# The first outer set of group 0 on raw x: layer normalisation moved behind four products' results

## Chip, cores and metric

The kernel runs on one core of a Trainium2 chip, in fp32. The metric is the device time of the whole program in microseconds, median over runs. The engines are TensorE (PE, with its weight loads PEld), VectorE (DVE), ScalarE (ACT), GpSimd (POOL) and the queue engine SyncE (SP), which here issues nearly all DMAs. Each engine works through its own instructions in the order in which the program issued them.

## The reference

`x` is 2048 rows (tokens) by 512 features. With LN(v) the row-wise normalisation without weights:

```python
xn = layernorm(x)                                   # (v - mean) / sqrt(var + 1e-5), per token
s  = xn @ (weight * block_mask).T                   # 512 x 512, 32 x 32 blocks kept or not
nx = xn * rsqrt(mean(xn * xn) + 1e-5) * ln_w
h  = silu(nx @ gate_w.T) * (nx @ up_w.T)            # 1792 inner features
g  = silu(h @ down_w.T)                             # back to 512
out = x + s * g
```

The kernel leaves the second (RMS) normalisation out of the products: its factor is applied to s at the end, and `ln_w` is multiplied into the weight tiles.

## The kernel before, in words

**Tiles.** P is 128, W is 512. The kernel works on transposed data: features on the 128 partitions, 512 tokens along a tile. x has four token groups t of 512 tokens (four tiles i of 128 tokens each) and four feature chunks c of 128. A product is one matmul of a 128x128 weight block by a 128x512 operand. All buffers in SBUF are slots of 128x512 in one large tile `mem`, cut into named rings; `F[...]` is the first slot of a ring.

**Strassen-like sets.** Gate and up weights are handled in seven groups g, and the masked 512x512 matrix is an eighth (g = G). Each group's product is a 2x2 block product, computed by seven block products ("outer" set q = 1, 2, 6, 5, 7, 3, 4), and each of those again by seven matmuls m (1, 5, 2, 6, 3, 7, 4 in order of issue). One pair (g, q) is an `instance`, and its number j is its place in the order: first (0,1), (0,2), (1,1), (1,2), (2,1) and so on, sets 1 and 2 of all groups, then the other five sets of each group. Instance 0 is (g=0, q=1), instance 1 is (0,2), instance 4 is (2,1).

**The order of work** is written out by hand: `at(pos, fn)` files a piece of work under a position, and at the end all pieces are issued in order of position. Instance j has its seven matmuls at positions 7j + (0, 2, 3, 4, 6, 8, 12), so neighbours interleave, and one position stands for 0.86 us. The dictionary `EARLY` moves single events of the first instances. `T(us)` turns a time into a position; it is written as a planned time of the head and only sets the order.

**An instance** (L333) adds its products up in three PSUM banks X, Y, Z. Bank X takes m = 1, 6, 7, 4 one after another and is read in between: after m = 1 (copied to seed Z, or, in the first instances, to a slot `s1`), after 6 (snapshot `s2`), after 7 (sum with `s5`, the result 3), after 4 (result 2). Bank Y takes m = 5 (snapshot `s5`) and 3. A matmul that adds into a bank waits for the reading before it. The snapshot or sum is a ScalarE copy if there is no prior tile, else a VectorE addition. PSUM has three X banks, two Y, one Z and two others (V), for transposes and gate values.

**The head.** `load_x(0)` brings the 512 tokens of t = 0 as four tiles, then come weight blocks `load_a` (L249) and the other tokens, all on SP's queue in that order; a one-column GpSimd copy (L685) makes the loads behind the first x tile wait for it. VectorE computes mean and variance (`stats`, L123), `factors` (L128) gives scl = 1/sqrt(var + eps) and nb = -mean * scl for each token, `normalise` (L142) applies them in place on ScalarE and VectorE, TensorE transposes 128x128 blocks (L155), and `evacuate` (L158) copies each PSUM bank to a `raw` slot on ScalarE. Weight blocks are multiplied by ln_w (`scale_a`, L266), and GpSimd forms their sums (`inner_a`, L312: s1, s2, s4, s3). `inner_b` (L211) forms the operands' differences for m = 5, 6, 7, 4, the first three on VectorE and the last on GpSimd. Until the first product TensorE multiplies the identity by itself (L702, 26 times).

**After sets 1 and 2 of a group** instance (g,1) has left its four tiles in `acc`, and (g,2), with `acc` as prior, its four in `c1`: the 2x2 results of gate (tiles 0, 1) and up (2, 3) for two token groups n. `done` (L420) then issues, for each n, a silu on ScalarE into a V bank, and `h_out` (L413), a VectorE multiplication of silu and up tile, followed by a store to `h_dram`. `acc` is stored to `acc_dram` and read back for the later sets of the group.

**At the end** x is added from `x_t`, the transposed x in memory, cut by rows and columns.

Of the kernel before, what the change touches and what calls it, by code (L numbers as in the profile page):

```python
# [31 lines left out]
def tile_masked_linear_gated_ffn(  # L32
# [21 lines left out]
    rms_dram = tc.dram_tile([NT], F32, name="rms_dram")  # L54
    acc_dram = tc.dram_tile([G + 1, P, 4, W], F32, name="acc_dram")
# [49 lines left out]
    keep = const.tile([P, 4, 16], F32, tag="keep", name="keep")  # L105

    def constants():
        make_identity(nc, ident)
        nc.gpsimd.memset(blockones, 0.0)
        for b in range(P // BLK):  # L110
            nc.gpsimd.memset(blockones[b * BLK : (b + 1) * BLK, b * BLK : (b + 1) * BLK], 1.0)


    xt, raw, stat = {}, {}, {}
    agg = small.tile([P, NTT, TT, 2], F32, tag="agg", name="agg", bufs=1)
    rms = small.tile([P, NTT, TT], F32, tag="rms", name="rms", bufs=1)

    def load_x(t):
        for i in range(TT):
            xt[t, i] = mem[:, first_slot[("B6", "vc", "v5", "B4")[t]] + i, :]  # L120
            nc.sync.dma_start(xt[t, i], x[(t * TT + i) * P : (t * TT + i + 1) * P, :])
# [6 lines left out]
    def factors(t):  # L128


        scl = small.tile([P, TT], F32, tag="scl", name=f"scl_{t}")
        nb = small.tile([P, TT], F32, tag="nb", name=f"nb_{t}")
# [193 lines left out]

    def weights(g, q, m):
        if q < 3 and m in (1, 2, 4):
            return aq[g, 0, q - 1][:, {1: 0, 2: 2, 4: 3}[m] * P :][:, :P]
        return aop[g, q][m]  # L330


    def instance(j, g, q, prior, dest, after):  # L333
# [4 lines left out]
        seeded = j > 1  # L338

        def mm(m, tag, key, first):  # L340
            if first and key not in st:
                st[key] = bank("Y" if key == "z" and j == 1 else tag, f"{key}_{j}")
            nc.tensor.matmul(st[key], weights(g, q, m), operand(q, m), start=first and not (key == "z" and seeded),  # L343
                             stop=True, skip_group_check=True)

        def seed():
# [4 lines left out]
            else:  # L351
                st["s1"] = slot("s2" if j else "s5", f"s1_{j}")
# [22 lines left out]
        at(EARLY.get((j, 0), 7 * j + 1), seed)  # L375
        for off, m, tag, first, snapshot, out in (
# [9 lines left out]
            at(EARLY.get((j, m), pos), mm, m, tag, key, first)  # L386
            if snapshot:
                at(pos + 1, snap, key, *snapshot)
            elif out:

                pos += 2.3 if prior is None and m == 2 and seeded else 1
                if m == 2:
                    pos = EARLY.get((j, "z"), pos)
                at(pos, total, key, *out)
                after(out[1], pos)


    def group(g, where):
# [56 lines left out]
        }  # L455
        for q in setup:
            instance(where[g, q], g, q, *setup[q])

# [7 lines left out]
        at(7 * where[g, 1] + 15, lambda: nc.sync.dma_start(acc_dram[g], sums))  # L466
# [91 lines left out]
    def load_final(R, Hh, i, slot_s, slot_x):  # L558
# [6 lines left out]
        nc.sync.dma_start(fin[m, t][1], x_t[m * P : (m + 1) * P, t * W : (t + 1) * W])  # L565
# [18 lines left out]
    def down_instance(o, q, where_, prior, dest, after):  # L584
# [78 lines left out]
        if last_set:  # L663
            at(where_(17) + 0.1, base_of_last)
            for part, pos in zip(parts, (where_(23), where_(24), where_(25))):
# [11 lines left out]
    T = lambda us: (us - 14.0) / 0.86  # L677
    EARLY.update({(0, 1): T(10.4), (0, 2): T(11.3), (1, 1): T(12.1), (1, 2): T(13.0), (0, 0): T(11.5), (1, 0): 4.3,
                  (0, "z"): 3.26, (1, "z"): 4.9})
    SILU = 26.2  # L680
    at(T(-10), constants)
    at(T(-10), load_x, 0)
    at(T(-10), lambda: nc.scalar.dma_start(lnw_sb, ln_w))

    at(T(-10), lambda: nc.gpsimd.tensor_copy(mem[:, F["a1"], 0:1], xt[0, 0][:, 0:1]))  # L685
    for K in range(2):
        at(T(-10), load_a, 0, K)
# [16 lines left out]
    at(T(1.4), lambda: warm(26, bank("V", "idle")))  # L704
    for t, p, step in ((0, T(7.1), 0), (1, T(12.5), 0), (2, 36.0, 1.2), (3, 36.1, 1.2)):
        plan(p, step, factors(t))
    for i in range(TT):
        half = act if i < 2 else dve
        at(T(3.7 + 0.82 * i), stats, 0, i)
        at(T(9.35 + 0.82 * i), stats, 1, i)  # L710
        for h, cols in enumerate((slice(0, W // 2), slice(W // 2, W))):
            at(T(7.95 + 0.9 * h + 0.4 * (i % 2)), normalise, 0, i, half, cols)
            at(T(13.45 + 0.9 * h + 0.4 * (i % 2)), normalise, 1, i, half, cols)
        for c in range(KC):
            at(T((8.9, 9.3, 9.8, 11.0)[c] + 0.05 * i), transpose, 0, c, (2, 3, 0, 1)[i], "XYYX"[c])
            at(T((14.35, 14.8, 15.25, 16.2)[c] + 0.05 * i), transpose, 1, c, (2, 3, 0, 1)[i], "XVVV"[c])
    at(T(6.0), scale_a, 0, 0, pool)
    at(T(6.1), scale_a, 0, 1, pool)
    for c in range(KC):
        at(T((9.75, 10.3, 10.85, 12.05)[c]), evacuate, 0, c, act)  # L720
        at((5.6, T(15.6), 6.0, 3.14)[c], evacuate, 1, c, act)
    for pos, q, m, eng in ((1.1, 1, 5, dve), (1.87, 1, 6, dve), (2.56, 1, 7, dve), (3.95, 2, 5, dve), (2.7, 1, 4, pool),
                           (4.6, 2, 6, dve), (7.2, 2, 7, dve), (5.0, 2, 4, pool)):
        at(pos, inner_b, q, m, eng)
    for q in (1, 2):
        for k in (0, 1):
            for n in (0, 1):
                at(8, outer_b, q, k, n, None)
    at(2.1, scale_a, 1, 0)
    at(5.2, scale_a, 1, 1)  # L730
    for i in range(TT):
        at(14.0 + 2.5 * i, stats, 2, i)
        at(25.0 + 3 * i, stats, 3, i)
        at((44.0, 51.0, 55.2, 58.2)[i], normalise, 2, i, act)
        at(40.5 + 2.4 * i, normalise, 3, i, dve)
    plan(36.2, 1.2, rms_factor())
# [24 lines left out]
    for g in range(G + 1):  # L761
# [8 lines left out]
        if g:  # L770
            plan(p - 7, 1, inner_a(g, 1))
        else:
            plan(T(9.9), 0, inner_a(0, 1, 0, 1))
            plan(T(11.9), 0, inner_a(0, 1, 1, 1))
# [150 lines left out]
```

## Time and profile before

| | us |
|---|---|
| median of 3 runs (lowest, highest) | 513.35 (513.21, 513.50) |
| profiled execution | 513.17 |
| its span, first to last instruction | 511.4 |
| TensorE busy (matmul records) | 505.8 |
| VectorE, ScalarE, GpSimd busy | 380.4, 182.6, 340.9 |
| warm-up on the identity | 1.35 to 10.3 |
| first product | 11.48 |
| DMA mean rate over the span | 238 GB/s |
| DMA rate 10 to 18 us, then 20 to 24 us | 377 to 404 GB/s, 0 |

How to read it: an fp32 product shows as two matmul records. Records overlap in the pipeline, so the sum of their durations is more than the time they take; what a product costs is read from the distance between starts. Names such as L97 are line numbers; L97 is the helper `add`, through which all elementwise sums go, so its rows are told apart by engine, tiles and shape. "idle before" is the time in which an engine stood still before an instruction, with what released it.

### The profile page before, as it was taken

The numbers are of one execution on the slowest core, as the hardware profiler recorded it, in microseconds if no ns is written. First come the engines' busy times: TensorE is split into PE (matmuls) and PEld (weight loads), VectorE is DVE, ScalarE is ACT, GpSimd is POOL, SyncE is SP. The second block draws the span as 40 slices with busy tenths as digits, with TensorE's granted clock in tenths as the row PEclk, the third lists the DMA queues.
The fourth block names the chain that finished last, engine by engine and source line by source line (L and its number), as shares of the span: only waits on it lengthen the run. The fifth ranks groups of instructions, "written<-read, shape, count | busy, mean of one in ns | idle before, by whom it ended". The sixth has DMA issues, their size and how long they took to land. (4 is left out here: it accounts for less than half of the span.)

```text
span 511.4 us, 4943 instructions
## 1 busy us (share of the span) xinstructions
PE 505.8 (99%) x1269; PEld 231.8 (45%) x1269; DVE 380.4 (74%) x590; ACT 182.6 (36%) x348; POOL 340.9 (67%) x283
## 2 busy tenths in 40 slices
PE   8999999999999999999999999999999999999997
PEld 8444444444444444444444444444444444444444
DVE  6878689876977969699696978968747645367736
ACT  4656754633536353353634433330100101001111
POOL 5522224994795968869597789976662754739960
PEclk9999999999999999999999999999999999999999
DMA  8436636369159386785948667499997698476472
GB/s 289 164 132 238 247 133 227 135 236 350 48 219 348 147 302 228 238 289 208 338 166 294 209 239 254 169 332 383 357 339 270 204 374 327 146 252 216 151 229 83
DMA packets 60460, 121.59 MB, mean 238 GB/s; under 512 B 5760, under 2 KB 13328, under 8 KB 58384
## 3 DMA queue, kind: packets, MB, share of 16 engines
q1 hardware_dynamic: 60288, 121.27, 66.8%
q8 instruction: 10, 0.16, 0.1%
q14 instruction: 18, 0.15, 0.1%
q10 hardware_dynamic: 144, 0.00, 0.0%
HBM read 75.11 MB, written 46.15 MB: 237 GB/s over the span
## 5 line engine op out<-in xcount | busy, mean ns | idle before, releaser
L97 POOL TENSOR_TENSOR mem<-mem 128x512 f32<-128x512 f32 (+4 forms) x245 | 305.2, 1267 | 135.4 <-ACT mem L264 36.5
L343 PE MATMUL x<-mem 128*128 128x512 f32 x448 | 213.6, 595 | 0.2 <-DVE mem L97 0.2
L343 PEld LDWEIGHTS x<-mem 128*128 128x128 f32 x448 | 83.7, 190 | 107.3 <-issue 86.9
L97 DVE TENSOR_TENSOR mem<-x,mem 128x512 f32<-128x512 f32 x137 | 92.5, 684 | 42.0 <-PE x L343 41.1
L343 PE MATMUL y<-mem 128*128 128x512 f32 x224 | 114.5, 593 | 0.3 <-DVE mem L97 0.3
L97 DVE TENSOR_TENSOR mem<-mem 128x512 f32<-128x512 f32 (+3 forms) x60 | 74.7, 1252 | 7.8 <-PE dx L591 4.3
L591 PE MATMUL dx<-mem 128*128 128x512 f32 x174 | 78.3, 592 | 0.0
L97 DVE TENSOR_TENSOR mem<-y,mem 128x512 f32<-128x512 f32 x96 | 65.6, 684 | 9.8 <-PE y L343 8.5
L343 PEld LDWEIGHTS y<-mem 128*128 128x128 f32 x224 | 42.2, 190 | 53.0 <-issue 47.8
L350 ACT COPY z<-x 128x512 f32<-128x512 f32 x54 | 30.9, 573 | 97.9 <-PE x L343 92.2
L343 PE MATMUL z<-mem 128*128 128x512 f32 x112 | 57.3, 593 | 0.0
L591 PEld LDWEIGHTS dx<-mem 128*128 128x128 f32 x174 | 33.1, 190 | 41.6 <-issue 40.4
L591 PE MATMUL dy<-mem 128*128 128x512 f32 x98 | 44.5, 592 | 0.0
L409 ACT ACTIVATE gate<-mem 128x512 f32<-128x512 f32 x56 | 33.1, 601 | 25.3 <-DVE mem L97 20.9
L414 DVE TENSOR_TENSOR mem<-gate,mem 128x512 f32<-128x512 f32 x56 | 38.0, 681 | 5.1 <-POOL mem L97 4.3
L564 POOL TENSOR_TENSOR mem<-mem 128x512 f32<-128x512 f32 x16 | 25.0, 1570 | 15.3 <-DMA mem<-s_dram 15.2
L343 PEld LDWEIGHTS z<-mem 128*128 128x128 f32 x112 | 21.0, 190 | 24.9 <-issue 23.9
L574 ACT ACTIVATE silu<-mem 128x512 f32<-128x512 f32 x15 | 9.0, 602 | 64.6 <-DVE mem L97 48.3
L97 DVE TENSOR_TENSOR mem<-z,mem 128x512 f32<-128x512 f32 x41 | 28.0, 682 | 3.5 <-PE z L343 3.5
L591 PEld LDWEIGHTS dy<-mem 128*128 128x128 f32 x98 | 18.6, 190 | 23.4 <-issue 23.4
L97 DVE TENSOR_TENSOR mem<-dx,mem 128x512 f32<-128x512 f32 x16 | 11.0, 690 | 20.1 <-PE dx L591 20.1
L591 PE MATMUL dz<-mem 128*128 128x512 f32 x56 | 25.2, 592 | 0.0
(73 smaller groups left out, 289.2 us busy)
## 6 DMA issues: line engine op xcount, KB each, us to landing
h_dram<-mem SPq DMA_DIRECT2D x98, 256.0 KB, 2.1
mem<-h_dram SPq DMA_DIRECT2D x28, 768.0 KB, 6.2
mem<-in_gu SPq DMA_DIRECT2D x42, 256.0 KB, 3.7
acc_dram<-mem SPq DMA_DIRECT2D x8, 1024.0 KB, 4.2
mem<-acc_dram SPq DMA_DIRECT2D x8, 1024.0 KB, 6.7
mem<-in_x SPq DMA_DIRECT2D x16, 256.0 KB, 5.2
s_dram<-mem SPq DMA_DIRECT2D x16, 256.0 KB, 4.8
mem<-s_dram SPq DMA_DIRECT2D x16, 256.0 KB, 6.3
```

The costliest lines, as they stand in the source:

```text
L97: eng.tensor_tensor(o, a, b, op)
L343: nc.tensor.matmul(st[key], weights(g, q, m), operand(q, m), start=first and not (key == "z" and seeded), stop=True, skip_group_check=True)
L350: nc.scalar.copy(st["z"], st["x"])
L409: nc.scalar.activation(gate[key], t(), AF.Silu)
L414: nc.vector.tensor_mul(a(), gate[key], b())
L564: at_later.append(lambda: nc.gpsimd.tensor_tensor(s_tile, s_tile, rms_bc[t], ALU.mult))
L574: nc.scalar.activation(b[0][:, part], y[:, part] if source is None else source(), AF.Silu)
L591: nc.tensor.matmul(st[key], w(), b(), start=first and key != "z", stop=True, skip_group_check=True)
```

## The change

Instance 0 no longer works on normalised x. `raw_x` loads four transposed tiles of x (chunks k = 0, 1 of token groups n = 0, 1) directly, `raw_t` forms their differences, and the seven matmuls multiply these. Because LN is per token, and tokens lie along the row of a result tile, the result of the scaled operand is the raw result times scl of the token, plus the row sum of the weights times nb of the token. So the four tiles of instance 0 (`p1`) are corrected afterwards: `sum_rows` computes the weight row sums on TensorE (the weight block times a column of ones), `fac_store` writes scl and nb of t = 0, 1 to memory and reads each back as a row spread over 128 partitions, and `raw_results` then, for each of the four tiles, multiplies by scl (GpSimd), adds the shift (computed on ScalarE into `tmp`), and adds the result to the tile of instance 1 (GpSimd). The silu and `h_out` of group 0's first set come after these. Instance 1 now has no prior, and x of t = 0, 1 is still normalised and transposed in the old way for it and all later instances.

With it go: other slots for x; `x_t` laid out in whole tiles; instance 2 takes the place of instance 1 as the last one that isn't seeded; both weight blocks of group 1 are scaled on GpSimd; the statistics of t = 2, 3 are later; a square root is computed at the very start; 8 warm-up products instead of 26 and 3 more later; the store of instance 0's tiles at position 38; and a new origin of T.

```diff
     def constants():
+        nc.gpsimd.memset(ones, 1.0)
+        nc.scalar.activation(root, ones, AF.Sqrt)
         make_identity(nc, ident)
...
     def factors(t):
-        scl = small.tile([P, TT], F32, tag="scl", name=f"scl_{t}")
-        nb = small.tile([P, TT], F32, tag="nb", name=f"nb_{t}")
+        if t < 2:
+            scl, nb = fac[:, 0, t, :], fac[:, 1, t, :]
...
+    def raw_x(k, n):
+        o = rop[k, n] = mem[:, RQ[2 * k + n], :]
+        nc.sync.dma_start(o, x_t[k, n])
+
+    def raw_t(m, eng):
+        b11, b12, b21, b22 = (rop[k, n] for k in (0, 1) for n in (0, 1))
+        o = rop[m] = mem[:, RQ[{5: 4, 6: 5, 7: 6, 4: 7}[m]], :]
+        a, b = {5: lambda: (b12, b11), 6: lambda: (b22, rop[5]), 7: lambda: (b22, b12), 4: lambda: (b21, rop[6])}[m]()
+        add(eng, o, a, b, ALU.subtract)
...
+    def sum_rows():
+        b = bank("V", "row_sums")
+        for r in range(2):
+            for c in range(2):
+                nc.tensor.matmul(b[:, r : r + 1], aq[0, 0, 0][:, (2 * c + r) * P :][:, :P], ones,
+                                 start=c == 0, stop=c == 1, skip_group_check=True)
+        held.append(b)
...
+    def fac_store():
+        b = bank("V", "fac_rows")
+        nc.tensor.transpose(b[: 4 * TT, :P], fac.rearrange("p a t i -> p (a t i)"), ident)
+        rows = small.tile([4 * TT, P], F32, tag="fac_rows", name="fac_rows", bufs=1)
+        nc.scalar.copy(rows, b[: 4 * TT, :P])
+        nc.sync.dma_start(fac_dram.rearrange("a t (i p) -> (a t i) p", p=P), rows)
+        for a in range(2):
+            for t in range(2):
+                nc.sync.dma_start(fac_bc(a, t), fac_dram[a, t].unsqueeze(0).to_broadcast([P, W]))
...
-        seeded = j > 1
+        seeded = j > 2
...
-            nc.tensor.matmul(st[key], weights(g, q, m), operand(q, m), start=first and not (key == "z" and seeded),
+            nc.tensor.matmul(st[key], weights(g, q, m), operand(q, m) if j else rop[{1: (0, 0), 2: (1, 0), 3: (1, 1)}.get(m, m)], start=first and not (key == "z" and seeded),
...
+    def raw_results(p1, c1, silu, h_out):
+        tmp = [mem[:, F["B7"] + k, :] for k in range(4)]
+        def shift(i):
+            r, n = divmod(i, 2)
+            nc.scalar.mul(tmp[i], fac_bc(1, n), row_sums[:, r : r + 1])
+        pos = CONVERT
+        for n in (0, 1):
+            for i in (n, n + 2):
+                at(pos + 0.5, shift, i)
+                at(pos, lambda i=i, n=n: add(pool, p1(i), p1(i), fac_bc(0, n), ALU.mult))
+                at(pos + 1.5, lambda i=i: add(pool, p1(i), p1(i), tmp[i]))
+                at(pos + 3, lambda i=i: add(pool, c1(i), c1(i), p1(i)))
+                pos += 4.5
+            at(pos + 0.2, *silu(n))
+            at(pos + 1.5, *h_out(n))
...
+        if g == 0:
+            p1 = tiles(R1)
+            setup.update({1: (None, p1, nothing), 2: (None, c1, nothing)})
...
-    T = lambda us: (us - 14.0) / 0.86
+    T = lambda us: (us - 11.4) / 0.86
+    EARLY.update({(0, 1): T(4.6), (0, 2): T(5.4), (0, 5): T(6.5), (0, 6): T(7.4), (0, 3): T(8.3), (0, 7): T(9.1), (0, 4): T(10.8),
+                  (0, "z"): T(13.7), (0, ("out", 7)): T(10.7), (0, ("out", 3)): T(14.5), (0, ("out", 4)): T(14.6),
+                  (1, 1): T(14.0), (1, 2): T(14.9), (2, 1): T(15.8), (2, 2): T(16.6), (1, 0): 8.6, (1, "z"): 9.5, (2, 0): 10.6,
+                  (2, "z"): 11.6, (1, "x"): 11.5})
+    SILU, CONVERT = 26.2, 14.5
...
+    at(T(-10), load_a, 0, 0)
+    for k, n in ((0, 0), (1, 0), (0, 1), (1, 1)):
+        at(T(-10), raw_x, k, n)
+    at(T(-10), lambda: nc.gpsimd.tensor_copy(mem[:, F["B6"], 0:1], rop[0, 0][:, 0:1]))
     at(T(-10), load_x, 0)
...
-    at(T(1.4), lambda: warm(26, bank("V", "idle")))
+    at(T(1.4), lambda: warm(8, bank("V", "idle")))
+    at(T(4.0), scale_a, 0, 0)
+    for us, m, eng in ((5.8, 5, dve), (6.6, 6, dve), (6.7, 7, pool), (6.8, 4, pool)):
+        at(T(us), raw_t, m, eng)
+    plan(T(4.9), 0, inner_a(0, 1, 0, 1))
+    at(T(10.9), sum_rows)
+    at(T(14.4), lambda: nc.scalar.copy(row_sums, held[0][:, :2]))
+    at(T(17.3), fac_store)
+    at(T(11.5), lambda: warm(3, bank("V", "idle")))
...
-        at(14.0 + 2.5 * i, stats, 2, i)
-        at(25.0 + 3 * i, stats, 3, i)
+        at(21.0 + 2.5 * i, stats, 2, i)
+        at(31.0 + 1.8 * i, stats, 3, i)
...
+        if g == 1:
+            plan(T(17.5), 0, inner_a(1, 1))
```

## The prediction

> **What bounds the kernel now.** I began with the page: TensorE (PE) is busy for 505.8 of 511.4 us.
>
> ```profile
> span 511.4 us, 4943 instructions
> PE 505.8 (99%) x1269; PEld 231.8 (45%) x1269; DVE 380.4 (74%) x590; ACT 182.6 (36%) x348; POOL 340.9 (67%) x283
> ```
>
> Part of that is warm-up on the identity, so I read the timeline of TensorE next: the warm-up, the first product, the first product after which nothing is missing, and the stretch at 46.59.
>
> ```profile
> 1.35 8.98 PE L702 MATMUL idle<-ident 128*128 128x128 f32 x52 [1.35 <-POOL ident masks.py:199]
> ...
> 11.48 1.10 PE L343 MATMUL x<-mem 128*128 128x512 f32 x2
> ...
> 24.27 1.02 PE L343 MATMUL y<-mem 128*128 128x512 f32 x2
> ...
> 46.59 1.88 PE L343 MATMUL x<-mem 128*128 128x512 f32 x4
> ```
>
> An fp32 product is two records; two products at 28.56, 31.14 and so on take 1.72 us to the next row, so a product costs 0.858 us, and a transpose (1.23 us for 11) 0.11. I call the row at 24.27 position 13. From there one product starts at each position of the written order: 24.27 + 0.858 x 27 = 47.44 for position 40, and the trace has it at 46.59 + 0.858 = 47.45. Of the time before 24.27, 11 products and 32 transposes are work (9.4 + 3.5 us); the other 11.4 us are a late start. That is all a better head can win. After it the only way to lose time is to make TensorE wait. So I read where the other engines stand in the stretch that the change fills:
>
> ```profile
> 20.88 4.26 POOL L97 TENSOR_TENSOR mem<-mem 128x512 f32<-128x512 f32 x5 [1.71 <-DVE mem L97]
> 31.63 3.02 POOL L97 TENSOR_TENSOR mem<-mem 128x256 f32<-128x256 f32 x4 [6.49 <-ACT mem L264]
> 44.10 3.05 POOL L97 TENSOR_TENSOR mem<-mem 128x256 f32<-128x256 f32 x4 [9.46 <-ACT mem L264]
> ```
>
> GpSimd is nearly free from 25 to 57 us: room. VectorE (DVE) is not: its timeline has no gap of note from 35.9 to 42 us, and its groups by shape give the prices:
>
> ```profile
> L97 POOL TENSOR_TENSOR mem<-mem 128x512 f32<-128x512 f32 x142 | 186.8, 1330 | 81.0 <-ACT mem L371 30.0 <-DVE mem L97 16.7 <-DVE mem L581 13.4
> L97 DVE TENSOR_TENSOR mem<-x,mem 128x512 f32<-128x512 f32 x137 | 92.5, 684 | 42.0 <-PE x L343 41.1
> L125 DVE BATCH_NORM_STATS2 st<-mem 128x6 f32<-128x512 f32 x16 | 10.8, 673 | 3.6 <-DMA mem<-in_x 3.6
> ```
>
> **What the Trainium skill says.** "TensorE: Matmul & The Clock Gate", Part 1, has TensorE at half rate until about 3.4 us of sustained work. The trace agrees in kind: warm-up records come every 0.214 us, and every 0.11 us after about 7.5 us, six microseconds in. "GPSIMD Engine Reference", section 4.1, calls two-input elementwise work about twice as slow there as on VectorE; here 1.28 to 1.33 us against 0.68. "DMA: Bandwidth & Descriptors", section "Anatomy of one DMA", gives a DMA about 2 us of fixed cost, mostly the receipt, and puts a wait on the issuing queue: a store followed by a load of the same rows pays it twice. Here an unhindered 256 KB store to h_dram lands after 2.0 to 2.3 us, the first x tile after 2.8.
>
> **The head, step by step.** Removed from the path: waiting for x, its statistics and its transposes before the first product. Added ahead of it: only the loads of the first weight block and of raw x.
>
> The weight block, first in SP's queue, lands at about 3.6 as the first x tile does now; ScalarE scales it in 2 x 0.46 to 4.5. The warm-up of 8 (16 x 0.214) ends at 4.8, and the first product starts there, 6.7 us earlier than now. At half rate it takes 1.7 us and the second most of that; with the clock changing at 7.5 as now, the second ends at about 7.9. Products 5, 6, 3, 7 follow to 11.3. Product 4 adds into a bank that VectorE must first read (0.65), so it ends at 12.9; if the clock changes 1.5 us earlier, at 12.2.
>
> load_x(0) waits on SP for the GpSimd copy that reads raw x, about 4.4; everything behind it on that queue is later too. Its first tile lands at 4.65 + 2.8 = 7.5, its last near 9.8 (0.69 us per 256 KB at some 380 GB/s), its statistics end at 10.6 and the factors wait behind the read of product 7. Normalising starts at 11.7 to 12.4, against 7.7 now; I take N = 12.1. From N on, in order of the queues: row sums and three warm-up products on TensorE to N+1.7; transposes to N+2.6; ScalarE, which first has four half tiles of 0.52, copies the banks to N+2.65 and N+3.2; products of the second set to N+4.4; second transposes and copies to N+6.0; two products of group 1 to N+7.2. VectorE meanwhile: two tiles, four statistics of 0.8, two sums of 0.6 to N+5.4; the square root waits for ScalarE until N+6.2; x of t=1 is normalised to N+9.3, transposed to N+9.0 (c=2,3), differenced, and product 5 of the second set starts at N+9.4. Two transposes of four and product 6 later, position 13 starts at N+12.0, about 24.1. By then 13 products are done, not 11: **gain 24.27 - 24.1 + 2 x 0.858, about 1.9 us** (1.6 to 2.3 by N; 3.4 if every event came at its planned time).
>
> **What the change adds on GpSimd.** raw_results is 12 tile operations (four multiplications, eight additions). At 1.26 us each (the pitch in the row at 20.88) they make 15.1 us, and inner_a of group 2, four times 0.75, lies among them: 18.1 us in one in-order queue. The plan spaces the twelve by 1.5 positions, 1.29 us, and leaves nothing for inner_a.
> It can start when the first broadcast row is there and when inner_b(1,4), ahead of it in the queue, is done. Row: fac is copied at N+7.8 = 19.9; its store waits on SP, and only load_a(3) and later loads, needed after 45 us, are behind it; it lands 2.1 to 2.5 later behind the last initial loads (18.1 now; plus 1.05 MB, 2.8 us, so 20.9), and the broadcast 2.8 after that: 25.3. inner_b(1,4): VectorE delivers inner_b(1,6) at N+12.9, plus 1.28: 26.3. So the chain runs from 26.3 to 44.4, h_out's first pair being ready after six operations and two of inner_a (9.1 us), at 35.4.
>
> **Who waits.** h_out is a VectorE instruction, written at positions 25 and 34. Without stalls these come at 32.5 and 40.2 (1.9 us before 34.57 and 42.3 of now). VectorE therefore stands still behind GpSimd twice, with its queue behind it. First: h_out, one z sum, the snapshot of x: product 7 of set 3 (position 29) starts at 35.4 + 0.6 + 0.6 + 0.68 = 37.3; unblocked it would be 36.1, now it is 38.0. Loss about 1.2. Second, and decisive: behind h_out(1) stand the last sum of set 3, two statistics, the y sum of set 4, another h_out and then the sum out of product 7, which product 4 of set 4 (position 40) must see done: 4 x 0.6 + 2 x 0.8 + 0.68, about 4.7 us. Position 40 starts at 44.4 + 4.75 = 49.15; now 47.45. That is 1.7 us late, the gain gone. VectorE then has 1.1 us of rms and factors, two snapshots and a sum queued, 3.0 us ahead of position 43, 2.6 us later: another 0.4.
> Sum: 513.17 (the profiled execution, span 511.4 and 1.8 around it) + 1.7 + 0.4 = 515.3; the median of the runs lies 0.18 above that execution: **515.4 us**. Everything later keeps its order and TensorE's pace, so the loss stays.
>
> **Costed at nothing.** Ones and the early square root: they lie beside the first loads (table load 1.16 to 2.44 already now). The four raw products' own differences: two on VectorE, which is idle until 7.5, two on GpSimd, done at 8.0 and 9.4; product 7, at 10.4, would wait if they were 2.4 us later. The four shifts on ScalarE (0.58 each): the first waits for the third broadcast, about 26.6, with the y snapshot for position 20 behind it; that has 0.6 us to spare. scale_a of group 1 moves to GpSimd, which has time until 18. 2 MB more DMA: statistics of x(2), x(3) come after 29 us. Contiguous x_t loads and the later acc store: same bytes. Unknown prices: N=1 row sums, not in the trace, 0.05 to 0.2 us a record (8); GpSimd at 1.26 to 1.33 is 0 to +0.8; a broadcast landing after 2.8 (idle queue) or 6.1 (the rms rows under full load) moves the start by nothing or +2.3.
>
> **Rivals.** *The head's gain is kept* (faster): VectorE doesn't hold TensorE up. For 1.9 us of gain position 40 must start at 45.5, so the chain must end by 40.8 and start by 22.7; the row's two DMA trips speak against it. If my reading of the queue is wrong, 510 to 512. *Even*: everything in the head comes at its planned time, the chain starts at its floor (row at 17.6, first broadcast 24.3), ends at 42.4, position 40 at 47.15, plus 0.4: 513.4. The present head runs about 1.1 us behind its plan at the transposes (planned 14.35, 15.43 in the trace), which speaks against it. *Worse*: broadcasts take 6 us, or TensorE falls back to half rate in the gaps of the head; the chain starts at 28.6 or later, and 517.7 to 520 follows.
>
> **How the numbers follow.** Forecast 0.58 (own range 514.0 to 517.3, chain start 25 to 27.5 and both GpSimd prices), gain kept 0.14, even 0.20, worse 0.08. Within 0.2% (about 1.0 us, what a measurement can tell here) is most of "even" and the lower edge of the forecast: 0.18 + 0.05. Slower 0.63, faster 0.14. The range 512.0 to 517.8 leaves out most of "gain kept" and "worse".
>
> **What would show it.** First product at 4.8; position 13 (the fifth product of set 1) near 24; GpSimd without a gap from about 26 to 44; the two h_out rows of group 0 on VectorE with idle time released by GpSimd, the second over 3 us; TensorE idle twice before an x product, released by VectorE. Wrong if VectorE's h_out doesn't wait, or if GpSimd's chain starts before 24.

## The result and the profile after

The changed kernel takes **518.95 us** (median; 518.74 to 519.54) against 513.33 for the kernel before, run beside it: ratio **1.0111, 95% interval 1.0094 to 1.0129**. The forecast was 515.4 with a range up to 517.8. It is slower, as forecast, but by 5.6 us where 2.0 were worked out.

The first lines of the page of the kernel after:

```profile
span 517.8 us, 4944 instructions
...
PE 504.8 (97%) x1248; PEld 228.1 (44%) x1248; DVE 380.3 (73%) x586; ACT 186.1 (36%) x356; POOL 361.4 (70%) x300
```

The span is 6.4 us longer while TensorE is busy 1.0 us less: it waits. (This execution took 519.54, 0.6 above the median.) The waits of TensorE in the kernel after, as total, count and longest, in us:

```profile
PE x L394 <- DVE mem L98: 4.0, 2, 2.6
PE x L394 <- DVE fac L145: 1.4, 1, 1.4
...
PE x L394 <- ACT mem L412: 0.7, 1, 0.7
PE pt L164 <- ACT mem L157: 0.6, 1, 0.6
```

Before, the only wait of note was the 1.3 us at the very start. Where they lie is in TensorE's timeline of the kernel after: warm-up, first product, position 13, position 29, position 40.

```profile
1.38 3.79 PE L783 MATMUL idle<-ident 128*128 128x128 f32 x16 [1.38 <-POOL ident masks.py:199]
4.96 1.71 PE L394 MATMUL x<-mem 128*128 128x512 f32 x2
...
27.26 1.02 PE L394 MATMUL y<-mem 128*128 128x512 f32 x2
...
42.15 1.13 PE L394 MATMUL x<-mem 128*128 128x512 f32 x2 [2.57 <-DVE mem L98]
...
53.25 1.13 PE L394 MATMUL x<-mem 128*128 128x512 f32 x2 [1.39 <-DVE mem L98]
```

The first product does start 6.5 us earlier than before (11.48), yet position 13 comes 3.0 us later (24.27). VectorE's timeline says what it waited for, in the head and at the two `h_out` of group 0 (L485):

```profile
9.26 0.69 DVE L131 BATCH_NORM_STATS2 st<-mem 128x6 f32<-128x512 f32 x1 [0.28 <-DMA mem<-in_x]
...
13.67 1.17 DVE L155 TENSOR_SCALAR mem<-mem,fac 128x512 f32<-128x512 f32 x2
...
20.95 0.18 DVE L145 RECIPROCAL fac<-fac 128x4 f32<-128x4 f32 x1 [1.23 <-ACT fac L149]
...
39.41 0.69 DVE L485 TENSOR_TENSOR mem<-gate,mem 128x512 f32<-128x512 f32 x1 [2.86 <-POOL mem L98]
...
48.51 0.69 DVE L485 TENSOR_TENSOR mem<-gate,mem 128x512 f32<-128x512 f32 x1 [2.01 <-POOL mem L98]
```

And GpSimd, whose chain follows the first operation of the second row, the last difference of instance 1 (`inner_b(1,4)`), without a gap:

```profile
25.44 1.27 POOL L98 TENSOR_TENSOR mem<-mem 128x512 f32<-128x512 f32 x1 [2.47 <-DVE mem L98]
28.90 22.62 POOL L98 TENSOR_TENSOR mem<-mem 128x512 f32<-128x512 f32 x21 [2.18 <-DVE mem L98]
```

**Where the 6.25 us of the profile went.** I split at position 13, and end at a product that both kernels have in the same place, the first z product behind four transposes after 50 us: 58.18 before, 64.43 after. From then on nothing more is lost: the last row of products starts at 503.96 and at 510.24, 6.28 apart. Before, position 13 to that product took 58.18 - 24.27 = 33.91 us; the changed kernel has two products fewer to do there, so 33.91 - 1.72 = 32.19 would be par. So the head loses 27.26 - 24.27 - 1.72 = **1.27** and the stretch behind it 64.43 - 27.26 - 32.19 = **4.98** (the two waits make 3.96; products that start 0.1 to 0.3 us late beside them, at 29.83 and at 55.07 make the rest).

### The profile page after: what moved, and what is told of

Its sections match the earlier page's. It is cut to its first block, busy times and chain, and to the rows that moved or that the text cites. A ratio compares the mean times of both kernels' runs of the same rounds, so it can differ in the third digit from the quotient of the medians.

```text
span 517.8 us, 4944 instructions
## 1 busy us (share of the span) xinstructions
PE 504.8 (97%) x1248; PEld 228.1 (44%) x1248; DVE 380.3 (73%) x586; ACT 186.1 (36%) x356; POOL 361.4 (70%) x300
## 5 line engine op out<-in xcount | busy, mean ns | idle before, releaser
L98 POOL TENSOR_TENSOR mem<-mem 128x512 f32<-128x512 f32 (+4 forms) x259 | 323.2, 1269 | 123.4 <-ACT mem L273 32.6
L98 DVE TENSOR_TENSOR mem<-x,mem 128x512 f32<-128x512 f32 x134 | 90.5, 684 | 39.4 <-PE x L394 35.8
L98 DVE TENSOR_TENSOR mem<-mem 128x512 f32<-128x512 f32 (+3 forms) x62 | 77.0, 1248 | 13.4 <-DMA mem<-in_x_t 6.5
L485 DVE TENSOR_TENSOR mem<-gate,mem 128x512 f32<-128x512 f32 x56 | 38.2, 682 | 9.5 <-POOL mem L98 9.2
L641 POOL TENSOR_TENSOR mem<-mem 128x512 f32<-128x512 f32 x16 | 25.7, 1614 | 13.6 <-DMA mem<-s_dram 13.5
L668 PEld LDWEIGHTS dy<-mem 128*128 128x128 f32 x98 | 18.6, 190 | 23.4 <-issue 23.2
```

The lines of the kernel that those rows point to most:

```text
L98: eng.tensor_tensor(o, a, b, op)
L485: nc.vector.tensor_mul(a(), gate[key], b())
L641: at_later.append(lambda: nc.gpsimd.tensor_tensor(s_tile, s_tile, rms_bc[t], ALU.mult))
L668: nc.tensor.matmul(st[key], w(), b(), start=first and key != "z", stop=True, skip_group_check=True)
```

## The experiments

The edits are told below. Head and later loss are worked out as just shown, from one profiled execution each. The last column is the median minus that of the kernel before, run beside it. One execution isn't the median: repaired_5's took 513.24, 0.63 under its median. repaired_4 and repaired_5 are the same program up to position 39, and their heads still differ by 0.43, so smaller differences between heads say nothing.

| kernel | position 13 | head | z product | behind it | sum | median |
|---|---|---|---|---|---|---|
| changed kernel | 27.26 | +1.27 | 64.43 | 4.98 | +6.25 | +5.62 |
| after_filled | 27.21 | +1.22 | 64.40 | 5.00 | +6.22 | +6.69 |
| chain_plus_two | 28.40 | +2.41 | 67.81 | 7.22 | +9.63 | +9.20 |
| hout_late_filled | 27.16 | +1.17 | 60.95 | 1.60 | +2.77 | +3.14 |
| no_correction | 26.31 | +0.32 | 58.79 | 0.29 | +0.61 | +1.27 |
| x_first | 27.55 | +1.56 | 61.81 | 2.07 | +3.63 | +3.66 |
| head_freed | 27.31 | +1.32 | 64.48 | 4.98 | +6.30 | +6.14 |
| repaired | 25.76 | -0.23 | 59.30 | 1.35 | +1.12 | +1.38 |
| repaired_2 | 25.04 | -0.95 | 59.28 | 2.05 | +1.10 | +1.92 |
| repaired_3 | 25.28 | -0.71 | 59.17 | 1.70 | +0.99 | +1.18 |
| repaired_4 | 24.95 | -1.04 | 58.82 | 1.68 | +0.64 | +1.11 |
| repaired_5 | 24.52 | -1.47 | 58.06 | 1.35 | -0.12 | +0.81 |

### Is it h_out's place in VectorE's queue?

hout_late files the same two silu and `h_out` of group 0 later; hout_late_filled and after_filled add seven warm-up products in the head to hout_late and to the changed kernel, so that TensorE doesn't idle there. (After idling it runs at half pace for a while in some executions: a product then takes 1.7 us; the last section shows it.)

```diff
-            at(pos + 0.2, *silu(n))
-            at(pos + 1.5, *h_out(n))
+            at((23.7, 34.2)[n], *silu(n))
+            at((30.05, 37.05)[n], *h_out(n))
```

```diff
+    at(T(9.2), lambda: warm(7, bank("V", "idle")))
```

> The changed kernel, with only the silu and h_out of group 0's first set issued later (h_out at positions 30.05 and 37.05 instead of 25 and 34), behind the sums of bank X. Theory 'queue' (VectorE stands still in h_out behind GpSimd's chain): TensorE's two idle times of 2.6 and 1.4 us go, the rest of the head stays; about 515.0 us, 4 under the changed kernel's 518.95. Rival 'head alone' (TensorE starts late, and the idle times would come back elsewhere, from the chain or the c1 slots): 518 to 519.

> The kernel with h_out later, and seven more products of the identity by itself between products 7 and 4 of the first set, where TensorE stood idle for some 2 us and its records came at half pace afterwards. Theory 'clock' (that idle time drops TensorE to half rate in part of the executions): no slow records in the head, position 13 near 27.2 us, 515.2 us with runs close together, against 515.8 to 518.9 before. If the slow records had another cause: 516.8 again.

> The changed kernel with the same seven products and nothing else. Its profile had no slow records, so theory 'clock' expects 518.7 with runs close together (nothing gained but the spread); if the drop is part of the changed kernel's median, 517 to 518. Against the run with h_out late and the same filler it gives the price of the wait in h_out without the clock: 3.4 us if the queue theory holds.

Measured: hout_late 516.76 (515.79 to 518.89), ratio 1.0071 [1.0044, 1.0098]; hout_late_filled 516.04 (515.24 to 516.13), 1.0060 [1.0045, 1.0075]; after_filled 519.59 (519.55 to 519.64), 1.0133 [1.0118, 1.0148]. The last two differ only in where the silu and `h_out` stand: **3.55 us**, where I expected 3.4. (Each of them lies 0.8 to 0.9 above what I expected for it; why was not followed.) TensorE's largest wait in hout_late_filled is

```profile
52.68 1.12 PE L394 MATMUL x<-mem 128*128 128x512 f32 x2 [0.89 <-DVE mem L98]
```

in place of 2.59 and 1.39 in after_filled. So the two waits were those of VectorE's queue behind `h_out`, as the prediction had them.

### Is it the correction, and does the chain's length pass through?

no_correction leaves out the eight multiplications and additions that scale and shift instance 0's tiles, and keeps the four additions to `c1`; the shifts are still computed, but nothing adds them, and the first set of group 0 is then not the reference's. chain_plus_two puts two idle multiplications on GpSimd ahead of the chain.

```diff
-                at(pos, lambda i=i, n=n: add(pool, p1(i), p1(i), fac_bc(0, n), ALU.mult))
-                at(pos + 1.5, lambda i=i: add(pool, p1(i), p1(i), tmp[i]))
```

```diff
+        for k in range(2):
+            at(pos - 0.1, lambda: add(pool, tmp[3], fac_bc(0, 0), fac_bc(0, 0), ALU.mult))
```

> The eight multiplications and additions of the correction on GpSimd are left out, so the first set's results are the raw products with only the four shifts added and no longer the reference's; everything else stays where it was put. The chain theory: GpSimd's chain is eight times about 1.2 us shorter, h_out finds its sums ready at 36 and 38, both waits of TensorE (2.57 and 1.39 us) go, and the time is that of the late places, about 515.2 to 516.0. If the time goes elsewhere, the waits stay or the time stays near 519.

> The changed kernel with two more GpSimd tile multiplications (of a row by itself into a scratch slot, results unchanged) ahead of the twelve of the correction. Theory 'queue': the chain ends 2.5 us later and TensorE's idle time grows by as much, 521.4 us. Rival 'head alone': the chain isn't what TensorE waits for, 519 us.

no_correction: 514.46 (513.97 to 515.33), ratio 1.0027 [1.0015, 1.0040]. Both waits are gone; its largest one is in the head, and the first of the two `h_out` waits 0.17 us:

```profile
PE x L394 <- DVE fac L145: 1.7, 1, 1.7
PE idle L781 <- POOL ident masks.py:199: 1.4, 1, 1.4
PE y L394 <- DVE mem L98: 0.5, 2, 0.3
```

```profile
35.77 0.69 DVE L483 TENSOR_TENSOR mem<-gate,mem 128x512 f32<-128x512 f32 x1 [0.17 <-POOL mem L98]
```

The correction's eight tile operations are thus what costs behind position 13: the loss there falls from 4.98 to 0.29 us, and the whole distance to the kernel before from 5.62 to 1.27. I had expected 515.2 to 516.0. (That the head too is better by 0.95 in this profile goes with x landing earlier in that execution; see the last section.)

chain_plus_two: 522.43 (521.35 to 523.01), 1.0174 [1.0156, 1.0191], 3.5 above the changed kernel. Two operations more, 2.5 us of GpSimd, add 2.24 us behind position 13 (7.22 against 4.98); the other 1.14 lie in the head, where TensorE ran at half pace for a while in this execution. TensorE in chain_plus_two, at the one long wait and just after:

```profile
45.40 2.07 PE L394 MATMUL x<-mem 128*128 128x512 f32 x2 [4.68 <-DVE mem L98]
47.26 1.91 PE L394 MATMUL y<-mem 128*128 128x512 f32 x2
48.97 1.40 PE L394 MATMUL z<-mem 128*128 128x512 f32 x2
```

The wait before the half pace is 2.11 longer than in the changed kernel (4.68 against 2.57), and so is VectorE's in front of the first `h_out` (4.97 against 2.86). The second `h_out` starts at 51.74, 2.09 later than there when the 1.14 of the head are taken off. So the chain's length does reach the end. With its products slowed, TensorE no longer comes early to the second wait.

### Why is the head late? What loads ahead of x cost

Three kernels add loads of 4 x 256 KB in front of x to the kernel before, which has none of the rest of the change. before_raw_loads takes rows out of the strided `x_t`; the other two take whole, contiguous tiles of x and lengthen the warm-up to 52 and to 44 products, to keep TensorE from idling.

```diff
+    for k in range(4):
+        at(T(-10), lambda k=k: nc.sync.dma_start(mem[:, F["B5"] + k, :], x[(12 + k) * P : (13 + k) * P, :]))
...
-    at(T(1.4), lambda: warm(26, bank("V", "idle")))
+    at(T(1.4), lambda: warm(44, bank("V", "idle")))
```

> The kernel before with four more loads of 256 KB (the raw x tiles, into slots that are free then and read by nobody) ahead of its loads of x. It prices the DMA part of the change alone. At the rate of the head (some 0.38 MB per us) they delay x by 2.8 us, and the whole kernel with it: 516.1. If the first microseconds run at a lower rate (0.28 MB per us), 3.7: 517.0. If x's arrival isn't what sets the head: 513.5.

> The kernel before with four more loads of 256 KB ahead of x, this time of contiguous rows of x (into free slots, read by nobody), and 52 warm-up products instead of 26, so that TensorE isn't idle before the transposes. The price of 1 MB of DMA alone: 2.8 us at 0.38 MB per us (516.1), 3.7 at 0.28 (517.0). The run before it (7 us) had rows cut at a stride and TensorE idle for 5 us; if these were not to blame, 520 again.

> The kernel before with four contiguous loads ahead of x and 44 warm-up products, which end as long after the factors (2.5 us) as in the kernel before; with 52 they ran on into the head. The pure price of 1 MB: x came 3.6 us later in that run, so 516.6 here; with 52 products it was 519.4.

Measured: before_raw_loads 520.26 (519.98 to 521.16), ratio 1.0137 [1.0122, 1.0152]; before_loads_filled 519.37 (518.30 to 519.57), 1.0130 [1.0113, 1.0147]; before_loads_44 517.57 (517.12 to 517.87), 1.0086 [1.0071, 1.0101]. In the first TensorE idles 4.97 us and then runs at half pace for a while; in the second the warm-up goes on until 14.5, a microsecond past the moment at which the transposes of the third begin. (before_loads_aligned, the second kernel once more, took 519.19, with position 13 another 0.9 later.) The last of the three is the clean one: **+4.5 us for 1 MB ahead of x**, 1.0 more than I expected. The first statistics of x on VectorE, in before_loads_44 and then in before_raw_loads, against 3.56 before:

```profile
7.12 0.69 DVE L125 BATCH_NORM_STATS2 st<-mem 128x6 f32<-128x512 f32 x1 [7.12 <-DMA mem<-in_x]
```

```profile
9.46 0.69 DVE L125 BATCH_NORM_STATS2 st<-mem 128x6 f32<-128x512 f32 x1 [9.46 <-DMA mem<-in_x]
```

3.56 us later for a contiguous megabyte, 5.90 for a strided one. Position 13, at 24.27 before, follows by 3.39 and 6.24, again in before_loads_44 and then in before_raw_loads:

```profile
27.66 1.02 PE L343 MATMUL y<-mem 128*128 128x512 f32 x2
```

```profile
30.51 1.02 PE L343 MATMUL y<-mem 128*128 128x512 f32 x2
```

In before_loads_44 the last row of products, too, is 3.43 later (507.39 against 503.96). The other 0.7 us of that execution lie behind the last VectorE instruction; their cause was not followed. The changed kernel has x's first statistics 5.70 later. Its raw products save so little because, in this order of loads, the raw tiles stand in front of x, and x's path leads to position 13.

### Gate, differences, order of loads

no_gate drops the one-column copy that holds x's loads back. diffs_apart exchanges GpSimd's two raw differences, so that VectorE's two run while GpSimd waits. head_freed does both, on after_filled. x_first loads x ahead of the raw tiles, without the copy, with the head's times written anew and the late `h_out`.

```diff
-    at(T(-10), lambda: nc.gpsimd.tensor_copy(mem[:, F["B6"], 0:1], rop[0, 0][:, 0:1]))
```

```diff
-    for us, m, eng in ((5.8, 5, dve), (6.6, 6, dve), (6.7, 7, pool), (6.8, 4, pool)):
+    for us, m, eng in ((5.8, 5, dve), (6.6, 6, dve), (6.7, 4, pool), (6.8, 7, pool)):
```

> The changed kernel without the one-column GpSimd copy that makes the loads of x wait for raw x. Theory 'x is late' (the head is set by the x tiles, which start 1.5 us later because of the wait and land 9.2 us after the start): the x tiles land about 1.2 us earlier, everything to the chain's start moves by that, and 517.7 us follows. Rival 'data rate' (the x tiles are late because 1.3 MB lie ahead of them, whenever they are issued): less than 0.4 us, 518.6 to 519. Rival 'processing order' (the head is set by VectorE's and ScalarE's queues): no change either.

> GpSimd's raw differences 4 and 7 change order, so that VectorE's two raw differences run while GpSimd waits for data. If the two engines slow each other, VectorE's two take about 1.5 us together in place of 2.47; the normalisation does not start earlier than x's tile allows, so the total stays near 519. If the differences are slow of themselves, they stay at 1.24 us each.

> The changed kernel with the filler products, without the one-column copy that holds back x's loads, and with GpSimd's raw differences 4 and 7 in the other order. If the gate and the slow differences together make x late, statistics start near 8.1 and normalising at about 12.5 in place of 13.6, position 13 comes 1.1 us earlier, the chain too, and the time is about 518.5. The rival, that later parts of the head (the third and fourth x tile, the square root behind the bank copies) set position 13, leaves 519.4 to 519.6.

> The changed kernel with x of t=0 loaded ahead of raw x and without the copy that made it wait, and the head's events written in the order that follows: statistics and normalisation of t=0 first, then the raw products, the statistics of t=1 straight after, 17 warm-up products, row sums in the gap before product 5, product 1 of the second set ahead of product 4 of the first; h_out at 30.05 and 38.05; factors of t=2, 3 at 37. Theory 'order of loads and queues' (the normalised path, not the raw one, sets the head, and every megabyte ahead of x costs 3.6 us): position 13 near 24.5, 1.5 us better than the kernel before counting the two products done early; 511.5 to 513. Rival 'the work itself' (one more megabyte and the correction can't be hidden anywhere): 514 or more.

no_gate: 519.26 (518.03 to 519.48), 1.0106 [1.0090, 1.0123], no change. My rival of the data rate would give that too, but the trace has another reason. x's first tile is issued at 3.06 and lands 4.6 us later, at 7.7, where the changed kernel issues it at 4.56 and has it at 9.2, also after 4.6. VectorE simply isn't there to take it. VectorE in no_gate:

```profile
6.42 2.53 DVE L98 TENSOR_TENSOR mem<-mem 128x512 f32<-128x512 f32 x2 [6.42 <-DMA mem<-in_x_t]
8.87 0.68 DVE L131 BATCH_NORM_STATS2 st<-mem 128x6 f32<-128x512 f32 x1
```

The two raw differences take 2.5 us, with a GpSimd difference running beside them from 7.17 in the changed kernel. In diffs_apart VectorE's two are done in 1.67, with GpSimd idle from 6.77 to 8.12, but there x isn't in yet:

```profile
6.37 1.67 DVE L98 TENSOR_TENSOR mem<-mem 128x512 f32<-128x512 f32 x2 [6.37 <-DMA mem<-in_x_t]
9.37 0.69 DVE L131 BATCH_NORM_STATS2 st<-mem 128x6 f32<-128x512 f32 x1 [1.33 <-DMA mem<-in_x]
```

The Trainium skill, "GPSIMD Engine Reference", section "Key points", has GpSimd share its SBUF interfaces with VectorE, with contention when a VectorE operation has two SBUF inputs. The traces agree: 1.24 us each with a GpSimd difference beside them, against 0.83 here and 0.71 in head_freed with GpSimd idle. But VectorE isn't always the one that pays. In hout_late, repaired, repaired_2 and no_correction, which keep the old order, VectorE's two take 1.55 to 1.81 us, and GpSimd's first difference takes 1.71 to 1.72 in place of 1.26. VectorE and GpSimd in hout_late (four small sums and both differences in one row):

```profile
6.33 1.55 DVE L98 TENSOR_TENSOR mem<-mem 128x512 f32<-128x512 f32 x2 [6.33 <-DMA mem<-in_x_t]
```

```profile
4.85 5.38 POOL L98 TENSOR_TENSOR mem<-mem 128x128 f32<-128x128 f32 x6 [0.20 <-ACT mem L273]
```

diffs_apart was run once and took 520.96, with TensorE at half pace from 15.4 to 18.6; 519 was expected.

head_freed: 519.20 (519.16 to 519.60), 1.0121 [1.0104, 1.0138]. The statistics begin at 8.39, 0.9 earlier, and still normalising starts at 13.57. My expectation fell. What holds it now is mainly the sum out of raw product 7, which stands between two steps of the factors in VectorE's queue; two small operations of the factors are also 0.2 and 0.3 us longer than in the changed kernel. VectorE and then TensorE (product 7) in head_freed:

```profile
11.72 0.38 DVE L148 TENSOR_SCALAR fac<-agg 128x4 f32<-128x4 f32 x1
12.27 0.69 DVE L98 TENSOR_TENSOR mem<-x,mem 128x512 f32<-128x512 f32 x1 [0.17 <-PE x L394]
```

```profile
11.10 1.13 PE L394 MATMUL x<-mem 128*128 128x512 f32 x2 [0.29 <-POOL mem L98]
```

Product 7 starts at 11.10 there, behind its operand, which the exchange has put second on GpSimd, and at 11.00 in the changed kernel. So the landing of x, the slow differences and the raw products' own end all meet near the same moment, and taking away one or two of them uncovers the next.

x_first: 516.77 (516.35 to 516.95), 1.0070 [1.0055, 1.0085], level with hout_late, whose late `h_out` it shares (the second one position later). My expectation of 511.5 to 513 fell; "the work itself" stands. The first product waits until 8.74. Normalising starts at 9.75, 3.9 us earlier than in the changed kernel, and position 13 comes at 27.55 all the same: TensorE stands in front of other operands, longest here.

```profile
21.68 1.10 PE L394 MATMUL x<-mem 128*128 128x512 f32 x2 [1.17 <-POOL mem L271]
```

That is a weight block which GpSimd scales behind its raw differences. So with x first it is no longer x of t = 0 that paces the head.

### Can the change be repaired?

repaired takes the late `h_out`, puts the row sums and four warm-up products ahead of normalising, moves the square root of t = 1 ahead of ScalarE's bank copies and the factors of t = 2, 3 behind the first sums of set 4 (one sum and the transpose of the rows move a little with them). repaired_2 also puts ScalarE's second halves of t = 0 (chunks 0 and 1) behind the bank copies of chunks 2 and 3, moves half a tile of t = 1 on VectorE, and puts these factors ahead of the sums, at 37.01; repaired_3 puts them at 39.5; repaired_4 adds head_freed's two edits; repaired_5 has them and the factors at 40.05 again.

```diff
-    at(T(10.9), sum_rows)
+    at(T(9.15), sum_rows)
...
-    at(T(11.5), lambda: warm(3, bank("V", "idle")))
-    for t, p, step in ((0, T(10.65), 0.1), (1, T(16.4), 0), (2, 38.2, 1.2), (3, 38.3, 1.2)):
+    at(T(9.2), lambda: warm(4, bank("V", "idle")))
+    for t, p, step in ((0, T(10.65), 0.1), (1, T(15.5), 0.05), (2, 40.05, 0.3), (3, 40.06, 0.3)):
```

> An attempt to keep the change and lose nothing: h_out later (30.05, 37.05), the weights' row sums and four products of the identity moved into TensorE's gap before product 4, the factors of t=1 and their square root ahead of the bank copies on ScalarE with the y sum of the first set moved into their wait, the rows' transpose behind one more normalised half, and factors and RMS of t=2, 3 from position 38 to 40. If the queues' order set the late head: position 13 near 25.3 us instead of 27.3, 513.3 us, level with the kernel before. If the head is set by DMA alone: 515.

> The repaired kernel (514.28) with three more moves: the bank copies of c=2, 3 on ScalarE ahead of the second halves of t=0, one half tile of t=1 on VectorE behind the first difference, and the factors and RMS of t=2, 3 at 37 with their second steps 1.3 and 2.6 positions later, so that ScalarE changes its table sooner. Position 13 near 25.2 instead of 25.76, and the small waits of TensorE between 48 and 55 us (1.0 in sum) mostly gone: 513.0. If these waits come from the work and not from its order: 514.

> The head is that of repaired_2; the factors and root mean squares of tiles 2 and 3 are put at position 39.5, behind the sums, in place of 37.01 ahead of them. If what repaired_2 lost after position 39 was the place of these operations (1.36 us of waiting at 49.25), this wait goes, the gain of position 13 (0.7 us over repaired) stays, and the time is about 513.6, 0.7 below repaired. The rival, that the first sums of set 3 come late whatever their neighbours, leaves 514.3 to 515.0.

> repaired_3 without the one-column copy and with the differences apart. If the head comes 0.8 to 1.1 us earlier and GpSimd's chain with it, the time falls from 514.4 to 513.3 to 513.6, level with the kernel before. The rival, that the loss after position 13 grows by what the head gains, leaves 514.4.

> repaired_4 with the factors and root mean squares behind the first x sum, at position 40.05 as in repaired. If these operations in front of that sum are what made TensorE wait 1.00 us at 50.91, this is 0.3 to 0.6 below repaired_4; if the wait only moves to the next snapshot, both are equal.

| | us | ratio |
|---|---|---|
| repaired | 514.28 (513.70 to 514.60) | 1.0026 [1.0016, 1.0036] |
| repaired_2 | 515.03 (514.41 to 515.49) | 1.0039 [1.0025, 1.0054] |
| repaired_3 | 514.37 (514.08 to 514.93) | 1.0025 [1.0016, 1.0033] |
| repaired_4 | 514.17 (513.54 to 514.84) | 1.0020 [1.0011, 1.0029] |
| repaired_5 | 513.87 (513.21 to 514.61) | 1.0016 [1.0009, 1.0022] |

None is faster than the kernel before. The head can be made to win: 1.04 us in repaired_4's execution and 1.47 in repaired_5's, with the same head. In repaired_5 position 13 comes 12.0 us after the start of normalising, as the prediction had it:

```profile
12.51 1.18 DVE L155 TENSOR_SCALAR mem<-mem,fac 128x512 f32<-128x512 f32 x2
```

```profile
24.52 1.02 PE L394 MATMUL y<-mem 128*128 128x512 f32 x2
```

But the stretch behind it gives 1.35 to 2.05 us back in every one of them, 0.29 without the correction. My expectation for repaired_3, 513.6, fell: the wait of repaired_2 in front of a y product went and came back in front of the next x product. TensorE in repaired_2 and in repaired_3, then VectorE in repaired_3:

```profile
49.25 1.12 PE L394 MATMUL y<-mem 128*128 128x512 f32 x2 [1.36 <-DVE mem L98]
```

```profile
50.91 1.12 PE L394 MATMUL x<-mem 128*128 128x512 f32 x2 [1.00 <-DVE mem L98]
```

```profile
46.58 0.69 DVE L485 TENSOR_TENSOR mem<-gate,mem 128x512 f32<-128x512 f32 x1 [0.56 <-POOL mem L98]
...
48.38 0.56 DVE L148 TENSOR_SCALAR scl<-agg 128x4 f32<-128x4 f32 x2
48.85 0.70 DVE L180 TENSOR_SCALAR rms<-agg 128x16 f32<-128x16 f32 x1
...
50.17 0.68 DVE L98 TENSOR_TENSOR mem<-x,mem 128x512 f32<-128x512 f32 x1
```

VectorE still waits for the chain once, and then the small operations stand ahead of the sum that position 43 needs. With them behind that sum (repaired_5) the median is 0.3 us lower, the lower edge of what I expected, but the runs of the two overlap widely, so this is weak evidence. For repaired_4 I had expected 513.3 to 513.6; the head gained 0.33, not 0.8 to 1.1.

## Why the prediction was wrong, step by step

**The first product, right.** 4.96 against 4.8.

**"Its first tile lands at 4.65 + 2.8 = 7.5": this step failed, and with it a term put at nothing.** The load is issued at 4.56, but lands after 4.6 us, at 9.2. The 2.8 was that of the first load of the whole program, on an idle queue (3.0 again for the first raw tile in the kernel after). When x's load is issued here, three raw tiles are still on their way; they land at 5.7, 6.4 and 7.1 (issued at 1.6, 2.1 and 2.6, landing 4.1, 4.3 and 4.5 later). So the statistics start at 9.26, and N, the start of normalising, is 13.67, not 12.1 and outside the 11.7 to 12.4 that I allowed: **+1.6**. The landing is not alone in this. VectorE's two raw differences, which I had costed at nothing, take 1.24 us each and end at 8.98, so a tile at 7.5 would have been taken up only 0.3 us sooner. In after_filled x was in at 8.5, the statistics followed the differences at 8.94, and N was 13.33. In repaired_2 the first tile did land at 7.5 and the differences were short, and N was 12.97, because the third tile took 4.6 us. In head_freed raw product 7 held N. How the 1.6 divides among the three is open: no run removes one of them alone and comes back to 12.1. The nearest is repaired_5, without the copy and with short differences, at 12.51.

**"Position 13 starts at N+12.0": failed as well, by 1.6**; it starts at N+13.6. Two terms were too small. Row sums and warm-ups, filed behind product 4, hold the transposes until 15.99, N+2.3, not N+1.7. The square root of t = 1 waits for ScalarE, which is copying banks, and runs at 20.70, N+7.0, not N+6.2 (its reciprocal is the row at 20.95). repaired moves both, with a sum and the transpose of the rows, and has N = 13.66 and position 13 at 25.76, 12.1 later; repaired_3, with more of ScalarE's work moved, 12.0. What each term costs by itself was not measured. VectorE in repaired, where normalising starts:

```profile
13.66 1.27 DVE L155 TENSOR_SCALAR mem<-mem,fac 128x512 f32<-128x512 f32 x2
```

Together the two misses turn the **gain of 1.9 into a loss of 1.27**, 3.2 us.

**The chain's start, 26.3: failed by what stands before it.** It waits for `inner_b(1,4)`, as predicted, whose end is 28.90 + 1.27 = 30.2. The broadcast rows, my other candidate, were issued from 24.22 on. The first of them, which the chain needs, landed after 3.1 us, at 27.3, so the rows were not the bound. (The first shift, which needs the third, ran at 29.28 after waiting 0.20 for it.) Of the 3.9 us, 3.2 are the two misses above and 0.7 come between position 13 and the chain.

**The chain's length, 18.1: right.** From 30.2 to the release of the second `h_out` at 48.5 it is 18.3.

**"About 4.7" behind the second `h_out`: right.** 48.51 to 53.25 is 4.74. The "another 0.4" after it: the four records at 55.07 and their successor cost 0.33 more than par. The first wait was worked out at 1.2 and is 2.57: the chain starts 2.9 us behind position 13, not 2.2, and between the first `h_out` (39.41) and the snapshot that TensorE waited for stands one statistics of 0.8 that I had overlooked.

So the mechanism behind the head was right in each step: GpSimd's chain, VectorE standing behind it twice, TensorE waiting twice in front of an x product. hout_late_filled and no_correction show it. Position 40 came at 53.25 and not at 49.15, mainly because what enters the chain was 3.9 us late. The sizes that failed are nearly all in the head; behind it they are the 0.7 before the chain and the overlooked statistics.

**The rivals.** "Gain kept" and "even" needed a chain that starts at 24.3 or earlier. "Worse" gave 517.7 to 520, where the result lies, and had 8 in 100; but neither of its causes is what happened in the profile after: the rows were not what the chain waited for, and TensorE shows no half pace between 13 and 27. The range was too narrow because N was given 0.7 us of play, though it rested on a landing time read from an empty queue and on a VectorE taken to be free.

## What to carry to other kernels

A load's landing time must be read from one that is issued into the same traffic: the same 256 KB landed after 2.8 us as the program's first load and after 2.9 to 4.6 behind three others, so give it a range. Starting TensorE earlier (here by 6.5 us) gains little when the operands of that early work are loaded and worked on ahead of the data that paces the rest; follow that data first. Work moved to an idle engine is not free if a busy engine's in-order queue waits for its results: file the consumer where the results will be, or take the work out, and count what stands behind the consumer.

## What the runs showed of the hardware that was not expected

**Half pace after short idling.** The Trainium skill, "TensorE: Matmul & The Clock Gate", Part 1, "What's actually happening", has TensorE fall back after an idle window of about 3.4 us, free-running. Here less than that came before half pace: 2.36 us of waiting. TensorE in hout_late, in an execution of 518.89 us:

```profile
13.40 2.04 PE L394 MATMUL x<-mem 128*128 128x512 f32 x2 [2.36 <-DVE fac L145]
15.24 1.71 PE L361 MATMUL row_sums<-ones,mem 128*128 128x1 f32 x8
```

A product takes twice its time and position 13 comes at 29.95. Waits of 2.60 us in no_gate (before 42.00) and of 2.58 in head_freed (before 42.22) were followed by it too, while waits of 2.57 and 2.59 in the changed kernel and after_filled were not. In diffs_apart and chain_plus_two it came in the head some 2 us after still shorter waits, of 1.72 and 1.04 us. TensorE in diffs_apart, where eight transposes take 1.91 us in place of 1.04:

```profile
13.52 1.12 PE L394 MATMUL x<-mem 128*128 128x512 f32 x2 [1.72 <-DVE mem L98]
...
16.78 1.91 PE L164 MATMUL pt<-ident,mem 128*128 128x128 f32 x8
```

With seven filler products in its head, hout_late's range of 515.79 to 518.89 becomes 515.24 to 516.13. The first change to full pace moves as well: the first product is 1.02 us wide in repaired_5 and 1.92 in repaired_3. So the price of a stall of this length is not one number, and these runs give no length of wait that is safe.

**Small VectorE operations beside GpSimd's.** The 128x4 and 128x16 operations of the factors and mean squares take 0.17 us in places and 0.45 to 0.70 in others (0.45 at 19.26 in the changed kernel, 0.70 in repaired_3's row at 48.85). GpSimd's row of tile operations runs from 26.92 to 49.52 in repaired_3; whether it is the cause was not separated.

**Landing times differ between executions.** Ten of these kernels have the same loads up to x's first tile. It landed 2.9 us after its issue in repaired_2's execution, 3.6 in no_correction's, 3.8 to 4.3 in six others, and 4.6 in the changed kernel's and diffs_apart's. So the head starts from data that can come 1.7 us earlier or later in kernels which differ only further on; part of no_correction's better head is that. The changed kernel's profile stands at the slow end.
